# A selective scan in four directions: where the transposed delta, the row and column sums and their timing come from

## The chip, the cores and the metric

The kernel is one launch of a program for one NeuronCore of a Trainium2 chip. It runs four layers, one after the other. The metric is the device time of that launch in microseconds (us). Two lengths occur below: the time of an execution as it is measured, and the span of the profile, from the first instruction to the last. The engines are named as in the profile: PE (TensorE, with PEld for its weight loads), DVE (VectorE), ACT (ScalarE), POOL (GpSimd) and SP (SyncE, which here only issues DMAs).

## The reference, cut to what matters

Only layer 0 is touched. Its input has B = 4 images of 64 x 64 tokens with 128 channels. A projection gives 2 x 256 channels; a depthwise 3 x 3 convolution with silu gives `xa`; from `xa` come a small rank-8 input of delta and 16 values B and C for each token. Then a selective scan runs over the 4096 tokens in four orders:

```python
x_t = jnp.transpose(xa, (0, 2, 1, 3)).reshape(b, L, D_INNER)
xs = jnp.stack([x_flat, x_t, jnp.flip(x_flat, 1), jnp.flip(x_t, 1)], axis=1)
...
delta = jax.nn.softplus(delta + delta_bias[None, :, None])
...
def step(h, inp):
    u_i, d_i, b_i, c_i = inp
    dA = jnp.exp(d_i[..., None] * A)
    h = h * dA + (d_i * u_i)[..., None] * b_i[:, None, :]
    y = jnp.einsum('gdn,gn->gd', h, c_i)
    return (h, y)
```

`u` is `xs`, so the inputs differ by order; delta, B and C are the same four times, in row order. The four results are turned back to image order and added, `4 * D * xa` is added, and a layer norm over the 256 channels, a product with `silu(z)` and an output projection follow. DI = 256 channels are two halves h of 128; NST = 16 states; TC = 64 tokens are a chunk, so that one image row or column is a chunk and there are 64 chunks.

## The kernel before, in words

The work on an image has stages, written as Python generators that can be run alone or a step (up to the next `yield`) at a time. `front` (L283) normalizes the input and applies the input projection; it sends the padded convolution input and silu(z) to DRAM. `middle` (L358) does, for each block of 512 tokens, the convolution of both halves (L369, from tiles that `shifted` loads, L346), the transposes of its result (L387), the projection to the rank-8 input, B and C (L402), B in token order (L417, L422) and delta with softplus (L428 to L446), and sends all that to DRAM. `back` (L450) reads the summed scans of a block, adds the row and column sums (L468), normalizes (L475 to L497), multiplies by silu(z) (L501) and projects out (L508, L512).

The scans are one loop of N = 512 chunks (L749): image b, half h of the channels, chunk c. 64 chunks, one image's half, are called a unit here. Image 0 goes through front and middle before the loop (L724, the prologue). Inside the loop the stages of the other images run beside the scans: from chunk c = 4 of h = 0, a generator chain runs `back` of the image before (at image 0 instead `spectra`, which prepares tables for a later layer), `front` of the next image, then, not before h = 1, `middle` of the next image. Each chunk calls `next(beside)` twice, after its first and after its second half. At c = 59 of h = 1 what is left of the chain is run to its end at once (L762, L763), because the next image's loads begin.

A chunk holds four scans: kp = 0 for row order, kp = 1 for column order, and j for forward and backward. Its two halves are kp = 0 and kp = 1. For each half:

- `products` (L631) multiplies the transposed delta times input, `du`, with a diagonal of B, `dg`, into two PSUM tiles `db` (three such tiles exist). Sixteen matmuls.
- `scan` (L645): for each j, DVE adds the carried state into the first column (L650) and runs the recurrence over 16 states x 64 tokens into `st`, a buffer of tag `big` of which three exist (L653). Then POOL makes the carry for the next chunk (L661) and multiplies the states by C in place (L669).
- `total` (L676) sums over the states on PE, with the 0/1 matrix `both`, in two parts of four states pairs, into `yp` (L682). After part 1, ACT copies the four results into `yr` (row orders) and `yc` (column orders), each 128 x 4096 (L701). In the later half of a unit, when a place has been written once, what lies there is first added by an identity matmul (L694). Rows go to DRAM from SP (L706); columns are added onto `y0` in DRAM by two accumulating DMAs of POOL at the unit's end (L710).

`du` needs delta in token order, times `xT`, which `fetch` (L565) reads from DRAM two chunks ahead into `xo`. Delta itself is read by channel (`dl`, L536), ACT reverses it (L599), PE transposes both (L617) into half of the PSUM tile `aux`, and two DVE operations multiply (L628).

The order on PE, ACT and DVE is the order of the program (`manual_schedule`, L748). For PE a chunk I is: products of its first half, `total(I - 2, 1)`, a background step, products of its second half, the delta transposes of chunk I + 1, a background step, `total(I - 1, 0)`. For DVE: two adds and scans of the first half, DVE work of a background step, `du` of the next chunk, two adds and scans of the second half, DVE work of a background step. On POOL every half's L661 and L669 stand in the same order with L550 (the first decay of a chunk, once in four chunks), L468, L501 and L710 between them.

Of the kernel before, what the change touches and what calls it, by code (L numbers as in the profile page):

```python
# [14 lines left out]
P = 128  # L15
B = 4
HW = 64
# [142 lines left out]
def layer0(cm, x, W, x1, also, kept):  # L160
# [5 lines left out]
    with ExitStack() as ctx:  # L166
# [4 lines left out]
        t4 = ctx.enter_context(tc.tile_pool(name="l0t4", bufs=4))  # L171
        p2 = ctx.enter_context(tc.tile_pool(name="l0p2", bufs=2))
# [32 lines left out]

        both = tl(wp, [P, TC], "both")
# [27 lines left out]

        yr = tl(wp, [P, S], "yr")
        yc = tl(wp, [P, S], "yc")

        aux = tl(pp, [P, 2, 2, P], "aux")
        yp = aux[:, 0].rearrange("p k (j t) -> p k j t", t=TC)
        pt2 = aux[:, 1]  # L240
# [19 lines left out]
        def begin(b):  # L260
            img[b] = {
                "zs": tl(dr, [P, 2, S], "zs"),
                "dl": tl(dr, [2, P, S], "dl_d"),
                "ct": tl(dr, [NST, S], "ct_d"),
                "xT": tl(dr, [2, S, P], "xT_d"),
                "y0": tl(dr, [P, 2, S], "y0_d"),
                "yr": tl(dr, [P, 2, S], "yr_d"),
            }
# [77 lines left out]
        def shifted(i, pool, tag):  # L346

            k, h = divmod(i, 2)
            x3 = tl(pool, [3 * CG, 4, 8 * PADW], tag, bufs=None if tag == "big" else 1)
            for dy in range(3):  # L350
                s0 = (8 * k + dy) * PADW
                nc.sync.dma_start(
                    x3[dy * CG : (dy + 1) * CG],
                    xc_d[4 * h : 4 * h + 4, :, s0 : s0 + 8 * PADW].rearrange("g p s -> p g s"),
                )
            return x3

        def middle(b, bank, pool, tag, ahead):  # L358

            ready = [shifted(i, pool, tag) for i in range(ahead)]  # L360
            for k in range(NBLK):
                cols = slice(k * BLK, (k + 1) * BLK)
                xa = []
                for h in range(2):
                    ps = bank()
                    x3 = ready.pop(0)
                    for dx in range(3):
                        for g in range(4):
                            nc.tensor.matmul(  # L369
                                ps[g * CG : (g + 1) * CG, :], lhsT=cdiag[:, 4 * h + g, dx, :],  # L370
                                rhs=x3[:, g, 0 : 8 * PADW].rearrange(
# [24 lines left out]
                    if h == 0:  # L396
                        yield
                        yield
# [49 lines left out]
                yield  # L448
# [82 lines left out]
        def load(q):  # L531
# [3 lines left out]
            dl = tl(p2, [P, QC * TC], "dl")  # L535
            nc.sync.dma_start(dl, img[b]["dl"][h, :, cols])  # L536
# [6 lines left out]
            return {"dl": dl, "dp": dp, "dA": dA[q % 2], "h": h}  # L543
# [21 lines left out]
        def fetch(I):  # L565
# [9 lines left out]
            xo = tl(p2, [P, 2, P], "xo", bufs=3)  # L575
            xT = img[b]["xT"][h]
# [12 lines left out]
            inp[I] = {"ct": ct, "xo": xo, "dg": dg}  # L589
# [4 lines left out]
        def start(I):  # L594
            b, h, c = place(I)
            q = {"c": c, "h": h, "w": quads[I // QC], **inp.pop(I)}
            dlc = q["w"]["dl"][:, c % QC * TC : (c % QC + 1) * TC]
            dlr = tl(p2, [P, TC], "dlr")
            nc.scalar.copy(dlr, dlc[:, ::-1])  # L599
            q["dl"] = dlc, dlr  # L600
            return q
# [11 lines left out]
        def delta(q):  # L613

            pt = pt2[:, q["c"] % 2]
            for j in range(2):
                nc.tensor.matmul(  # L617
                    pt[j * TC : (j + 1) * TC, :], lhsT=q["dl"][j], rhs=cm.ident,
                    start=True, stop=True,
                )  # L620
            q["pt"] = pt

        def inputs(q):

            q["du"] = []
            for kp in range(2):
                d_ = tl(p2, [P, P], f"du{kp}")
                nc.vector.tensor_tensor(d_, q["xo"][:, kp, :], q["pt"], ALU.mult)  # L628
                q["du"].append(d_)

        def products(q, kp):  # L631
            bs = [tl(db, [P, 2 * NH0, TC], "db") for _ in range(2)]
            for g in range(2):
                for j in range(2):
                    half = slice(j * TC, (j + 1) * TC)
                    for p in range(2):
                        nc.tensor.matmul(  # L637
                            bs[j][p * TC : (p + 1) * TC, g * NH0 : (g + 1) * NH0, :],
                            lhsT=q["du"][kp][half, g * TC : (g + 1) * TC],
# [5 lines left out]
        def scan(I, q, kp, bs, st, old, new):  # L645
            c = q["c"]
            for j in range(2):
# [11 lines left out]
            us = slice(2 * kp, 2 * kp + 2)  # L659
# [16 lines left out]
        def total(I, part):  # L676
            b, h, c = place(I)
            st = states[I]
            late = c >= NCHUNK // 2
            for n in range(4 * part, 4 * part + 4):  # L680
                for p in range(2):
                    nc.tensor.matmul(  # L682
                        yp[p * TC : (p + 1) * TC], lhsT=both,
                        rhs=st[:, :, p * NH0 + n, :], start=(n == 0),
                        stop=(n == NH0 - 1 and not late),
# [3 lines left out]
            vs = [views(yc if kp else yr, c)[2 * j + kp] for j in range(2) for kp in range(2)]  # L689
            for j in range(2 if late else 0):  # L690

# [1626 lines left out]
```

## Time and profile before

| what | value |
|---|---|
| three runs | 10992.04, 11000.42, 11008.0 us; median 11000.42 |
| the profiled execution | 10974.05 us, span 10972.3 us |
| mean granted TensorE clock | 0.898 |
| first scan starts, last scan starts | 281.70 us, 6368.6 us |
| busy over the span | PE 9474.1, DVE 7569.2, POOL 5331.9, ACT 5425.1 us |
| busy from 280 to 6385 us | PE 5453, DVE 5423, POOL 5080, ACT 3066 us |
| HBM read, written | 667.01 MB, 331.61 MB |

The loop of layer 0 fills slices 2 to 23 of the page's 40. A line of the page's fifth part reads: source line, engine, operation, output <- inputs by the program's names with shapes, count | busy us, mean ns of one | idle us of that engine just before them, and what ended most of it. A line of the timeline reads: start, length, engine, source line, operation, names, shapes, count, and in brackets the idle time before it and what ended it.

### The profile page before, as it was taken

To read this page: it belongs to the slowest core of one execution; us is meant where nothing else is said; L and a number is where in the kernel's file an instruction comes from. 1 tells how busy PE (TensorE), PEld (TensorE's weight loads), DVE (VectorE), ACT (ScalarE), POOL (GpSimd) and SP (SyncE) were. 2 spreads that over 40 slices of the span, in tenths; PEclk is the share of its full clock that TensorE was granted. 3 is DMA by queue.
4 is the path that set the end of the run, shared out by engine and by line. 5 is a ranking of instruction groups with operands and counts; after the bars stand their busy time and mean duration, and the time that the engine had idled before them with its cause. 6 is when DMAs were issued, how large, how long until landed. Compare 5 with 4: busy or idle time off the path is not lost. (4 is left out here: it accounts for less than half of the span.)

```text
span 10972.3 us, 163387 instructions
## 1 busy us (share of the span) xinstructions
PE 9474.1 (86%) x59368; PEld 4529.1 (41%) x59368; DVE 7569.2 (69%) x11174; ACT 5425.1 (49%) x13536; POOL 5331.9 (49%) x2581
## 2 busy tenths in 40 slices
PE   6789998889998899998889954999999956988886
PEld 2344444344443344443344432444444434544442
DVE  1898988888988898988899966545452122355546
ACT  6666543555544564545542223777776622433321
POOL 0788888878888888887889940000000000000000
PEclk7899999999999899998999977999999976677777
DMA  5334443334443334443333341111100065022101
GB/s 147 106 107 149 131 128 114 109 109 149 136 132 116 107 117 151 135 122 113 109 106 99 103 120 36 41 35 35 39 24 17 16 191 104 17 46 56 37 24 46
DMA packets 1471160, 1009.46 MB, mean 92 GB/s; under 512 B 697540, under 2 KB 1296296, under 8 KB 1466008
## 3 DMA queue, kind: packets, MB, share of 16 engines
q1 hardware_dynamic: 1468056, 982.24, 30.3%
q0 software_dynamic: 2304, 16.78, 0.7%
q8 instruction: 475, 7.78, 0.3%
q14 instruction: 325, 2.66, 0.1%
HBM read 667.01 MB, written 331.61 MB: 91 GB/s over the span
## 5 line engine op out<-in xcount | busy, mean ns | idle before, releaser
L653 DVE TENSOR_TENSOR_SCAN big<-dA,db 128x1024 f32<-128x1024 f32 x2048 | 4680.0, 2286 | 82.1 <-ACT dA L560 3.2
L669 POOL TENSOR_TENSOR big<-big,ct 128x2048 f32<-128x2048 f32 x1024 | 4646.1, 4537 | 85.0 <-DVE big L653 5.4
L637 PE MATMUL db<-dg,du 64*64 64x512 f32 x16384 | 2442.7, 617 | 101.1 <-DVE db L650 87.8
L682 PE MATMUL aux<-big,both 128*64 128x256 f32 x16384 | 2104.0, 401 | 407.1 <-DVE db L650 260.6
L682 PEld LDWEIGHTS aux<-big,both 128*64 128x64 f32 x16384 | 1202.8, 142 | 1396.1 <-issue 622.9
L701 ACT COPY yr<-aux 128x64 f32<-128x64 f32 x1024 | 226.6, 222 | 2668.6 <-PE aux L694 1250.7
L637 PEld LDWEIGHTS db<-dg,du 64*64 64x64 f32 x16384 | 748.2, 135 | 1321.2 <-issue 1218.4
L608 ACT ACTIVATE dg<-mask,BT 128x64 f32<-128x64 f32 x4096 | 1007.4, 341 | 4.0 <-DMA dg_d<-dg 4.0
L1441 PE MATMUL av<-e,x 128*128 128x512 f32 x2048 | 974.0, 592 | 4.6 <-ACT e L1436 4.6
L1392 PE MATMUL qk<-a,xT 128*128 128x512 f32 x2048 | 966.6, 594 | 8.6 <-ACT e L1396 7.8
L1396 ACT ACTIVATE e<-qk,nk 128x512 f32<-128x512 f32 x1024 | 692.9, 685 | 539.2 <-PE qk L1392 538.4
L560 ACT ACTIVATE dA<-dp,A 128x252 f32<-128x252 f32 x2048 | 870.5, 509 | 1.4
L971 POOL TENSOR_TENSOR g_rs<-g_rs,qrow 128x4 f32<-128x4 f32 x32 | 41.1, 1285 | 1499.9 <-DVE g_rs L970 1499.9
L661 POOL TENSOR_TENSOR cy<-big,a 128x32 f32<-128x32 f32 x1008 | 272.8, 271 | 821.7 <-DVE big L653 524.4
L1392 PEld LDWEIGHTS qk<-a,xT 128*128 128x128 f32 x2048 | 378.0, 190 | 462.3 <-issue 358.0
L1441 PEld LDWEIGHTS av<-e,x 128*128 128x128 f32 x2048 | 381.6, 190 | 434.7 <-issue 393.6
L1436 ACT ACTIVATE e<-e 128x1024 f32<-128x1024 f32 x510 | 538.7, 1056 | 15.3
L1917 ACT ACTIVATE e<-s 72x576 f32<-72x576 f32 x448 | 273.3, 642 | 492.0 <-PE s L1910 489.0
L628 DVE TENSOR_TENSOR du<-xo,aux 128x128 f32<-128x128 f32 x1024 | 248.2, 284 | 379.5 <-PE aux L617 286.2
L650 DVE TENSOR_TENSOR db<-db,cy 128x16 f32<-128x16 f32 x2016 | 336.9, 167 | 202.0 <-PE db L637 184.2
L1928 POOL COPY vp<-vt 72x160 f32<-72x160 f32 x56 | 19.6, 352 | 890.8 <-PE po L1934 874.4
L2150 DVE SCALAR_TENSOR_TENSOR tex<-x,gw,tex 128x128 f32<-128x128 f32 x768 | 264.5, 344 | 256.1 <-PE x L2144 241.2
(525 smaller groups left out, 10869.4 us busy)
## 6 DMA issues: line engine op xcount, KB each, us to landing
ct<-ct_d SPq DMA_DIRECT2D x1024, 128.0 KB
dg_d<-dg SPq DMA_DIRECT2D x256, 512.0 KB
dg<-dg_d SPq DMA_DIRECT2D x256, 512.0 KB
xo<-xT_d SPq DMA_DIRECT2D x2048, 32.0 KB
x<-xc_d SPq DMA_DIRECT2D x144, 264.0 KB
dp<-dl_d SPq DMA_DIRECT2D x256, 128.0 KB
t2k<-in_x SPq DMA_DIRECT2D x96, 256.0 KB
sp<-sp_d SPq DMA_DIRECT2D x16, 1280.0 KB
```

What stands on the lines that cost most here:

```text
L560: nc.scalar.activation(w["dA"][:, :, g, n, 1:], w["dp"][:, g, :, 1:], AF.Exp, scale=A[:, w["h"], g, n : n + 1],)
L608: nc.scalar.activation(q["dg"][:, n, :], mask, AF.Copy, scale=BT[:, q["c"], n : n + 1])
L637: nc.tensor.matmul(bs[j][p * TC : (p + 1) * TC, g * NH0 : (g + 1) * NH0, :], lhsT=q["du"][kp][half, g * TC : (g + 1) * TC], rhs=q["dg"][ha ...
L650: nc.vector.tensor_tensor(bs[j][:, :, 0], bs[j][:, :, 0], old[:, u, :], ALU.add)
L653: nc.vector.tensor_tensor_scan(st[:, u].rearrange("p n t -> p (n t)"), q["w"]["dA"][:, c % QC].rearrange("p g n t -> p (g n t)"), bs[j].re ...
L669: nc.gpsimd.tensor_tensor(sv, sv, q["ct"].rearrange("p n t -> p (n t)").unsqueeze(1) .to_broadcast([P, 4, NH0 * TC]), ALU.mult,)
L682: nc.tensor.matmul(yp[p * TC : (p + 1) * TC], lhsT=both, rhs=st[:, :, p * NH0 + n, :], start=(n == 0), stop=(n == NH0 - 1 and not late),)
L1392: nc.tensor.matmul(ps, lhsT=me["xT"][:, kt * P : (kt + 1) * P], rhs=me["a"][k], start=True, stop=True,)
L1396: nc.scalar.activation(e[:, j, :], ps, AF.Exp, bias=me["nk"][:, kt : kt + 1], scale=2.0)
L1436: nc.scalar.activation(es[g + 2], es[g + 2], AF.Exp)
L1441: nc.tensor.matmul(avs[b, k], lhsT=img[b]["x"][:, kt, :], rhs=e[:, j, :], start=(kt == 0), stop=(kt == NT - 1),)
L1917: nc.scalar.activation(e.rearrange("p j h q -> p j (h q)"), ss[p][0:HALF, :, 0 : 2 * WIN], AF.Exp, scale=0.5,)
```

## The change

- `middle` makes delta in token order itself: after softplus, four transposes, a copy by ACT and a store to a new DRAM tensor `dT`; a matmul with `flip` reverses the tokens within each chunk, with another copy and store for the backward scans. A block has 15 steps instead of 12 (two empty steps and the last one are dropped).
- `fetch` reads `dT` into `dt`, with two DMAs; the load of `dl`, ACT's reversal, the transposes and their PSUM tile are gone. `du` of both halves is one DVE operation of 2 x 128 elements, with `dt` repeated over kp.
- `yr` and `yc` of 4096 tokens become `ys`: two buffers each of eight rows at either end, and of half a unit's columns. They are stored every eight chunks (rows) and every 32 (columns). In the later half of a unit POOL's accumulating DMAs add the rows in DRAM, as they do for the columns; the identity matmuls are gone.
- Both parts of `total(I - 2)` run in chunk I, each half a chunk later than before.
- The convolution's input comes in two tiles of half the size (of the tag `t4k`), two steps ahead, with six DMAs for three; the chain beside the scans starts at c = 5 instead of 4; `spectra` uses part of `padded[0]` as its input tile.

```diff
+        yb = ctx.enter_context(tc.tile_pool(name="l0y", bufs=2))
...
+        flip = tl(wp, [P, P], "flip")
+        nc.vector.memset(flip, 0.0)
+        for p in range(2):
+            half = slice(p * TC, (p + 1) * TC)
+            nc.vector.tensor_copy(flip[half, half], cm.ident[half, half][:, ::-1])
...
-        yr = tl(wp, [P, S], "yr")
-        yc = tl(wp, [P, S], "yc")
-
-        aux = tl(pp, [P, 2, 2, P], "aux")
-        yp = aux[:, 0].rearrange("p k (j t) -> p k j t", t=TC)
-        pt2 = aux[:, 1]
+        yp = tl(pp, [P, 2, 2, TC], "yp")
...
+                "dT": tl(dr, [2, 2, S, P], "dT_d"),
...
-            x3 = tl(pool, [3 * CG, 4, 8 * PADW], tag, bufs=None if tag == "big" else 1)
+            x3 = [tl(pool, [3 * CG, 2, 8 * PADW], tag) for _ in range(2)]
...
-                    if h == 0:
-                        yield
-                        yield
...
                     nc.sync.dma_start(img[b]["dl"][h, :, cols], r)
-                yield
+
+                    yield
+                    ps = bank()
+                    for i in range(4):
+                        nc.tensor.transpose(
+                            ps[:, i * P : (i + 1) * P], r[:, i * P : (i + 1) * P], cm.ident
+                        )
+                    for j in range(2):
+                        t = tl(tmp, [P, 4, P], "t2k")
+                        nc.scalar.copy(t, ps.rearrange("p (t c) -> p t c", c=P))
+                        nc.sync.dma_start(
+                            img[b]["dT"][h, j, cols, :].rearrange("(t p) c -> p t c", p=P), t
+                        )
+                        yield
+                        if j == 0:
+                            ps = bank()
+                            nc.tensor.matmul(
+                                ps, lhsT=flip, rhs=t.rearrange("p t c -> p (t c)"),
+                                start=True, stop=True,
+                            )
...
-            dl = tl(p2, [P, QC * TC], "dl")
-            nc.sync.dma_start(dl, img[b]["dl"][h, :, cols])
...
+            dt = tl(p2, [P, P], "dt", bufs=3)
+            nc.sync.dma_start(
+                dt[0:TC], img[b]["dT"][h, 0, c * TC : (c + 1) * TC, :]
+            )
+            nc.sync.dma_start(
+                dt[TC:P], img[b]["dT"][h, 1, c * TC : (c + 1) * TC, :]
+            )
...
-            q["du"] = []
-            for kp in range(2):
-                d_ = tl(p2, [P, P], f"du{kp}")
-                nc.vector.tensor_tensor(d_, q["xo"][:, kp, :], q["pt"], ALU.mult)
-                q["du"].append(d_)
+            q["du"] = tl(p2, [P, 2, P], "du")
+            nc.vector.tensor_tensor(
+                q["du"], q["xo"], q["dt"].unsqueeze(1).to_broadcast([P, 2, P]), ALU.mult
+            )
...
+            if part == 0:
+                if c % 8 == 0:
+                    for i in range(2):
+                        ys[i] = tl(yb, [P, 8 * TC], f"yr{i}")
+                if c % (NCHUNK // 2) == 0:
+                    ys[2] = tl(yb, [P, HW, TC], "yc")
...
-            for j in range(2 if late else 0):
-
-                for kp in range(2):
-                    v = vs[2 * j + kp]
-                    nc.tensor.matmul(
-                        yp[:, kp, j, :], lhsT=cm.ident, rhs=v[:, ::-1] if j else v,
-                        start=False, stop=(j + kp == 2),
-                    )
...
+            if r == 7:
+                for i, r0 in enumerate((c - 7, NCHUNK - 1 - c)):
+                    to = img[b]["yr"][:, h, r0 * TC : (r0 + 8) * TC]
+                    if c < NCHUNK // 2:
+                        nc.sync.dma_start(to, ys[i])
+                    else:
+                        nc.gpsimd.dma_start(to, ys[i], accum_op=ALU.add)
+            if c % (NCHUNK // 2) == NCHUNK // 2 - 1:
...
-                if h == 0 and c == 4:
+                if h == 0 and c == 5:
...
-                            middle(b + 1, own_bank, p2, "x3", 1),
+                            middle(b + 1, own_bank, t4, "t4k", 2),
...
                 if I > 1:
-                    total(I - 2, 1)
+                    total(I - 2, 0)
...
                 if nxt:
-                    delta(nxt)
                     inputs(nxt)
                 scan(I, now, 1, bs, st, carry, new)
...
-                if I:
-                    total(I - 1, 0)
+                if I > 1:
+                    total(I - 2, 1)
```

## The prediction

> **What bounds the kernel now.** I read the page's groups first, for the loop of layer 0 (512 chunks; first scan 281.7 us, last ends 6370.9, so 6089 of the 10972 us span). Only this loop and the prologue before it change.
>
> ```profile
> L653 DVE TENSOR_TENSOR_SCAN big<-dA,db 128x1024 f32<-128x1024 f32 x2048 | 4680.0, 2286 | 82.1 <-ACT dA L560 3.2
> L669 POOL TENSOR_TENSOR big<-big,ct 128x2048 f32<-128x2048 f32 x1024 | 4646.1, 4537 | 85.0 <-DVE big L653 5.4
> ...
> L628 DVE TENSOR_TENSOR du<-xo,aux 128x128 f32<-128x128 f32 x1024 | 248.2, 284 | 379.5 <-PE aux L617 286.2
> ```
>
> A chunk needs four scans on DVE and two multiplies on POOL, and the two engines are almost equally full. Then the waits inside the loop (engine and line, waited for: us, times, longest):
>
> ```profile
> DVE du L628 <- PE aux L617: 286.2, 265, 15.1
> DVE db L650 <- PE db L637: 184.2, 62, 17.9
> ```
> ```profile
> PE aux L682 <- POOL big L669: 112.5, 23, 7.5
> ```
> ```profile
> ACT yr L701 <- DMA yr_d<-yr: 69.7, 6, 21.0
> ```
>
> So DVE loses about 600 us to lateness of others, and L628, the line that changes, is where most of it shows. Next the timeline of a chunk with nothing beside it:
>
> ```profile
> 6001.43 4.53 POOL L669 TENSOR_TENSOR big<-big,ct 128x2048 f32<-128x2048 f32 x1
> ...
> 6003.59 2.29 DVE L653 TENSOR_TENSOR_SCAN big<-dA,db 128x1024 f32<-128x1024 f32 x1
> ...
> 6005.95 0.26 POOL L661 TENSOR_TENSOR cy<-big,a 128x32 f32<-128x32 f32 x1
> ...
> 6006.03 0.48 DVE L628 TENSOR_TENSOR du<-xo,aux 128x128 f32<-128x128 f32 x2 [0.15 <-PE aux L617]
> 6006.29 4.52 POOL L669 TENSOR_TENSOR big<-big,ct 128x2048 f32<-128x2048 f32 x1
> 6006.43 0.18 DVE L650 TENSOR_TENSOR db<-db,cy 128x16 f32<-128x16 f32 x1
> ```
>
> Starts to starts: add and scan 2.40 us, four of them 9.60; the two du 0.40; waits 0.25: a quiet chunk takes 10.29 (3 to 62 of the last unit of 64). POOL's pair L661, L669 runs back to back in 4.83 (6001.08 to 6005.95 is one of them), 9.66 a chunk. When DVE reaches du, POOL is still in L669 of the half before, by some 0.2 us.
>
> [...] Today du reads one operand from PSUM. After the change both lie in SBUF. The trace agrees, with a group that has two SBUF inputs already:
>
> ```profile
> 394.30 4.50 POOL L669 TENSOR_TENSOR big<-big,ct 128x2048 f32<-128x2048 f32 x1
> ...
> 395.55 3.53 DVE L862 SCALAR_TENSOR_TENSOR t4k<-t4k 128x256 f32<-128x256 f32 x1
> ...
> 399.01 0.17 DVE L650 TENSOR_TENSOR db<-db,cy 128x16 f32<-128x16 f32 x1
> ```
>
> L862 has 256 elements and takes 3.52 to 3.73 us all eight times, ending 0.27 us after POOL's multiply. [...] L856, the same shape with POOL free, takes 399 to 422, and DVE's next one starts 0.32 after it. [...] here L710 keeps POOL 0.86 to 1.19 us each.
>
> **The change part by part** (64 chunks are a unit, eight units).
>
> Delta from memory: four PE transposes (0.37 us of PE), one ACT copy and the wait L617 go. SP gets two issues a chunk for dt and loses one per four chunks. xo's four take 2.5 to 5.5 us of SP in the timeline, so two more of the same size take 1.2 to 2.8; in a quiet chunk SP stands idle 2.8 (6013.54 to 6016.32). They are asked for two chunks ahead, so I take nothing; uncovered they cost what xo costs du now, 22 us. In the middle SP also gets three more loads per half block and four stores of dT a block, behind which the fetches of later chunks are queued; they have the same chunk of room. One du of 256 elements for two: 0.40 to 0.32.
>
> The lock, quiet chunk: du right behind a scan waits for the end of L669 (0.2) and 0.2 to resume. Following both engines round from a du that ends at 0: DVE is back at the next du at 9.6; POOL starts its first multiply at 0.27, the second pair follows at 0.27 + 4.83, its end is at 9.6 or little after, and du resumes 0.2 behind it and takes 0.2: 10.05. POOL's L550 (0.41, once in four chunks) now delays du too: 10.1 against 10.29. A price of nothing would be 9.97.
>
> The lock, behind other DVE work: where a background operation stands between the second scan and du, POOL has started its next multiply.
>
> ```profile
> 2452.64 0.67 DVE L291 BATCH_NORM_STATS2 gn_st<-bg 128x6 f32<-128x512 f32 x1
> 2452.80 0.26 POOL L661 TENSOR_TENSOR cy<-big,a 128x32 f32<-128x32 f32 x1 [0.51 <-DVE big L653]
> 2453.14 4.54 POOL L669 TENSOR_TENSOR big<-big,ct 128x2048 f32<-128x2048 f32 x1
> 2453.23 0.47 DVE L628 TENSOR_TENSOR du<-xo,aux 128x128 f32<-128x128 f32 x2
> ```
>
> Here du, reading PSUM, runs through the multiply; with two SBUF inputs it would stand until 2457.7, 4.65 in all. I count 12 such places each for L291 and L512, 12 for L480 (4.07 left), 4 for L865/L868 (4.65). L291 and L512 miss the gap by 0.02 to 0.09 us only, so I take half of theirs. Three softplus operations (2.1) fall there in 20 of the new blocks of 15 steps (12 steps before): 3.1 each.
>
> POOL's debts. POOL's delays no longer spread over half a chunk: du hands them to DVE. In "back", per block of 512 tokens, L468 waits for its load (up to 4.7) and takes 2.36: 2.4 on DVE; with that debt open L480 costs 3.3 more in the other half of cases; L501 3.0. Per block: own DVE work 6.7 + 2.4 + 3.7 + 1.2 + 0.3 + 3.0 = 17.3. The sums, put half a chunk later, take away what costs as much today: PE waiting for L669 (some 5 us a block), with the products of the next chunk queued behind it and DVE behind those. Nothing takes its place on PE: L669 has half a chunk more. If POOL were a whole half behind, the wait would be back. The scans' third buffer is now free only after the last sum, but the products of the same chunk stand behind that sum on PE anyway.
>
> Sums in memory: yr, yc get two buffers. The stall at each unit's third chunk (24 to 28 us instead of 10; the seven du waits of 12.6 to 15.1) goes, 99 us, and so do the late ident matmuls L694 (1.06 of PE a chunk). But 64 row transfers move from SP to POOL, and 16 more of yc: 80 x 1.1 = 88, all before a du; where the middle runs POOL has slack: 70. L669 and L661 queue behind them.
>
> Middle: two more transposes and a flip per half, PE 14 us per 7.5 chunks instead of 11 per 6, the same density. Convolution 2.72 + sums 1.88 + products 1.88 exceed DVE's 4.8 plus du by 1.3, twice a block (today 1.8 to 2.9). 10.1 + (4.5 DVE + 2.6)/7.5 = 11.05 a chunk.
>
> The burst: the middle has 15 steps x 8 blocks = 120 instead of 96, and a chunk takes two. Back (89 steps) begins at chunk 5, front has 51, so in units 3 and 5 the middle begins at chunk 11; by chunk 59, where the loop at L763 empties the rest at once, 96 steps are done and 24 are left, in series through one PSUM bank. One softplus chain is 9.2 us in the prologue's timeline (L428 at 238.6 to L446's end at 247.8), and about 3.8 for transposes, copy, flip and copy: two of them 26. A whole block adds convolutions 2 x 6, and 5 to 6 for L402 and L417: 44. Together 70, and 5 for waits between them: 75, with DVE and POOL empty; 5 more for the slow PE after it (PE's twelve matmuls take 3.68 instead of 1.95 us after a gap). Unit 1 has two steps left, 5.
>
> Now the units, after against before (unit lengths from first scan to first scan). Unit 0: 8 quiet chunks 81, spectra 404 (392 now, less 0.2 a chunk, plus its four locks), front 272: 757 to 763. Unit 1: 59 middle chunks 652, softplus locks 25, burst 5, 5 quiet chunks: 732 to 747. Units 2 and 4: 5 quiet chunks 50, 45 of back 454 and 8 x 17.3 = 138, front 151: 794 to 811 and 807; 6, without front, 784 to 791. Units 3 and 5: 11 chunks 111, 48 of middle 549 with locks, burst 80, 5 chunks 50: 790 to 746 and 750. Unit 7: 64 quiet ones, 646 to 674. Sum 6087 against 6089. Then POOL's transfers +70, the prologue +36 (its ACT, 18.6 us busy of 24.7 a block, gets four copies of 0.56, and the softplus chain grows; between 18 and 80), one more sum after the last chunk +2. That is +108 on the profiled execution's 10974.05 (span 10972.3 and 1.75 around it): 11082. The median of the runs stands 26 above it: **11108**.
>
> **Rivals.** A, on the other side: du is let in. If the lock waits behind background work don't happen[...], the terms for L291, L512, L480, spectra and softplus go, 190 us: 10918. It decides at the order of du and L669 after a scan; for it speaks the margin of under 0.1 us, against it L862. C: the lock costs nothing anywhere, nor do debts pass through it: 6 to 7% of the loop, 10640; L862 speaks against. B: worse than forecast: all of L291 and L512 (+56), bursts of 100 (+40), prologue at its upper bound (+44): 11250.
>
> **How the numbers follow.** Forecast 0.58, A 0.22, C 0.04, B 0.16. About 0.2% (22 us) can be told from no change. A and C are faster, 0.26; of the forecast 0.08 falls within 0.2%; slower 0.66. The range leaves out C and a little at either end: 10890 to 11270.
>
> **What would show it.** Right: du waiting on POOL L669 instead of PE, single du of 3 to 5 us behind L291, L480, L442; quiet chunks of 10.1; no stall at a unit's third chunk; a hole of 75 us in the scans at chunk 59 of units 3 and 5; POOL DMA issues x96. Wrong: quiet chunks at 9.97 or above 10.3, du under 0.5 us behind background work, no hole.

## The result, and the profile after

The changed kernel takes 11441 us (median of 4 runs, 11427 to 11461); the kernel before took 10998 on the same chip (4 runs). The ratio is 1.040, 95% interval 1.038 to 1.042: slower by 443 us. The prediction had 11108 with a range of 10890 to 11270. The direction was right, the size a quarter of what came.

Nearly all of it lies where the change is. The first scan comes at 406.1 us instead of 281.7 (+124, forecast +36), and the loop takes 6422 us instead of 6089 (+333, forecast +70). What follows the loop takes 4603 against 4601.

The groups of the page of after (out<-in, busy us, mean ns of one, idle time ahead and what ended most of it). Scan and multiply are what they were; du is 546 us instead of 248, though half as many:

```profile
L663 DVE TENSOR_TENSOR_SCAN big<-dA,db 128x1024 f32<-128x1024 f32 x2048 | 4679.5, 2286 | 86.1 <-PE db L646 7.7
L678 POOL TENSOR_TENSOR big<-big,ct 128x2048 f32<-128x2048 f32 x1024 | 4652.7, 4544 | 107.6 <-PE db L646 27.3
...
L636 DVE TENSOR_TENSOR du<-xo,dt 128x256 f32<-128x256 f32 x512 | 546.2, 1067 | 34.0 <-DMA xo<-xT_d 16.7
```

The waits of after inside the loop, to be set against those of before. du's 286 us of waits for PE are gone, but L660, one step further down VectorE's queue, waits 417 instead of 184 for the products:

```profile
DVE db L660 <- PE db L646: 417.0, 175, 16.8
...
PE db L646 <- DMA dg<-dg_d: 118.4, 28, 12.3
PE bg L453 <- DVE t2k L447: 116.5, 30, 8.1
...
PE yp L698 <- ACT yc L712: 72.9, 31, 6.6
...
DVE db L660 <- POOL cy L670: 53.6, 13, 12.1
```

In the page's way of attributing, PE is late for three reasons that the forecast had at nothing: a load of dg that lands late, transposes of dT behind VectorE's softplus, and the sums behind ScalarE's copies.

A fourth stands in the groups of the page. The same 16384 products take PE 2809 us instead of 2443 (after, then before):

```profile
L646 PE MATMUL db<-dg,du 64*64 64x512 f32 x16384 | 2809.2, 649 | 602.9 <-DVE db L660 453.1
```
```profile
L637 PE MATMUL db<-dg,du 64*64 64x512 f32 x16384 | 2442.7, 617 | 101.1 <-DVE db L650 87.8
```

The granted TensorE clock over the loop is 0.905 in after and 0.951 in before (0.929 in e1 and 0.955 in e11 below). In these two traces it is either full or half. 1624 of the products of after begin at half clock, 631 of those of before; at half clock one takes 1057 ns (median), at full clock 589. Where the clock fell, PE had mostly stood: it was busy 33% of the 4 us ahead of such a fall in after (mean of 146), and 86% of the whole loop; in before 31% (67 falls) and 89%. So in these traces waits of PE are followed by slower products. The prediction had this cost for the holes only (5 us); what it makes of the 443 was not measured apart.

A quiet chunk of unit 7, in the timeline of after. From the scan at 6500.86 to the one four scans on, at 6511.04, it is 10.18 us (median of the unit 10.12, forecast 10.1); du takes 0.64 because it stands until 0.28 after the end of POOL's multiply:

```profile
6498.89 4.54 POOL L678 TENSOR_TENSOR big<-big,ct 128x2048 f32<-128x2048 f32 x1
...
6500.86 2.29 DVE L663 TENSOR_TENSOR_SCAN big<-dA,db 128x1024 f32<-128x1024 f32 x1
...
6503.07 0.64 DVE L636 TENSOR_TENSOR du<-xo,dt 128x256 f32<-128x256 f32 x1
6503.38 0.45 POOL L670 TENSOR_TENSOR cy<-big,a 128x32 f32<-128x32 f32 x1
```

Where a background operation stands between the second scan and du, POOL has begun its next multiply, and du stands through it, as forecast. Here L293 (L291 of before) is that operation. du ends at 2674.18, 0.29 after L678:

```profile
2668.80 0.70 DVE L293 BATCH_NORM_STATS2 gn_st<-bg 128x6 f32<-128x512 f32 x1
...
2669.36 4.53 POOL L678 TENSOR_TENSOR big<-big,ct 128x2048 f32<-128x2048 f32 x1
2669.42 4.76 DVE L636 TENSOR_TENSOR du<-xo,dt 128x256 f32<-128x256 f32 x1
2674.10 0.17 DVE L660 TENSOR_TENSOR db<-db,cy 128x16 f32<-128x16 f32 x1
```

And the hole at the 59th chunk of unit 3: three stretches of after by busy time of PE, its weight loads, VectorE, ScalarE and POOL. In the middle one the steps that are left run in series, and VectorE works 8.94 of 80 us. Unit 5 has the same hole.

```profile
3471.00:3555.00 84.00, 75.31 (x554) 31.71 (x554) 76.45 (x70) 35.02 (x82) 68.03 (x31) 0.96 0.46 129
3555.00:3635.00 80.00, 39.59 (x144) 13.38 (x146) 8.94 (x15) 35.05 (x48) 6.45 (x5) 0.55 0.36 106
3635.00:3700.00 65.00, 62.87 (x428) 24.29 (x426) 64.17 (x56) 25.09 (x99) 58.58 (x26) 1.00 0.27 79
```

The units against what the prediction gave them (us from first scan to first scan; the last runs to the end of the loop; the forecast's +70 for POOL's transfers isn't in its units):

| unit | 0 | 1 | 2 | 3 | 4 | 5 | 6 | 7 |
|---|---|---|---|---|---|---|---|---|
| before | 763 | 747 | 811 | 746 | 807 | 750 | 791 | 674 |
| forecast | 757 | 732 | 794 | 790 | 794 | 790 | 784 | 646 |
| after | 804 | 775 | 845 | 855 | 828 | 860 | 800 | 655 |

Unit 7, with nothing beside it, is nearly right. Every unit with work beside it is 16 to 70 us above forecast, 3 and 5, where the middle runs, by most.

### The profile page after: what moved, and what is told of

It is laid out like the page before. It is cut to its first block, busy times and chain, and to the rows that moved or that the text cites. A ratio compares the mean times of both kernels' runs of the same rounds, so it can differ in the third digit from the quotient of the medians.

```text
span 11431.0 us, 156940 instructions
## 1 busy us (share of the span) xinstructions
PE 9610.5 (84%) x55656; PEld 4238.1 (37%) x55656; DVE 7843.6 (69%) x10665; ACT 5419.6 (47%) x13149; POOL 5455.5 (48%) x2661
## 5 line engine op out<-in xcount | busy, mean ns | idle before, releaser
L678 POOL TENSOR_TENSOR big<-big,ct 128x2048 f32<-128x2048 f32 x1024 | 4652.7, 4544 | 107.6 <-PE db L646 27.3
L646 PE MATMUL db<-dg,du 64*64 64x512 f32 x16384 | 2809.2, 649 | 602.9 <-DVE db L660 453.1
L698 PE MATMUL yp<-big,both 128*64 128x256 f32 x16384 | 2188.0, 413 | 81.8 <-ACT yc L712 72.9
L698 PEld LDWEIGHTS yp<-big,both 128*64 128x64 f32 x16384 | 1175.3, 147 | 1450.1 <-issue 832.3
L712 ACT COPY yr<-yp 128x64 f32<-128x64 f32 x1024 | 224.9, 220 | 1670.4 <-PE yp L698 1669.7
L670 POOL TENSOR_TENSOR cy<-big,a 128x32 f32<-128x32 f32 x1008 | 341.6, 339 | 1250.3 <-DVE big L663 945.1
L660 DVE TENSOR_TENSOR db<-db,cy 128x16 f32<-128x16 f32 x2016 | 334.5, 166 | 472.1 <-PE db L646 417.0
L636 DVE TENSOR_TENSOR du<-xo,dt 128x256 f32<-128x256 f32 x512 | 546.2, 1067 | 34.0 <-DMA xo<-xT_d 16.7
```

Source lines behind the costliest of these rows:

```text
L636: nc.vector.tensor_tensor(q["du"], q["xo"], q["dt"].unsqueeze(1).to_broadcast([P, 2, P]), ALU.mult)
L646: nc.tensor.matmul(bs[j][p * TC : (p + 1) * TC, g * NH0 : (g + 1) * NH0, :], lhsT=q["du"][half, kp, g * TC : (g + 1) * TC], rhs=q["dg"][ha ...
L678: nc.gpsimd.tensor_tensor(sv, sv, q["ct"].rearrange("p n t -> p (n t)").unsqueeze(1) .to_broadcast([P, 4, NH0 * TC]), ALU.mult,)
L698: nc.tensor.matmul(yp[p * TC : (p + 1) * TC], lhsT=both, rhs=st[:, :, p * NH0 + n, :], start=(n == 0), stop=(n == NH0 - 1),)
```

## Experiments

The theory after this reading: the loss is the sum of several separate things that "delta by way of memory" brings: the lock on du (a du of over 1 us ends only 0.28 to 0.29 us after POOL's multiply beside it), DMA issues on SP's queue, work in series in the two holes and in the prologue, and PE waiting for VectorE's softplus. The rivals: that one of them is nearly all of it, or that they hide each other, since one late engine covers another. Most kernels undo one thing or leave one out; e5, e6 and e11 go back to delta by PE with the rest of the change kept, and e9 combines four repairs. Since the times of before differ by up to 0.3% from chip to chip, the column to read is the difference to the kernel before on the same chip.

| run | us | before there | difference | ratio, 95% | first scan | loop |
|---|---|---|---|---|---|---|
| after | 11441 | 10998 | +443 | 1.038 to 1.042 | 406 | 6422 |
| e1, du reads PSUM | 11175 | 10986 | +189 | 1.016 to 1.020 | 409 | 6141 |
| e2, no dT made beside the loop | 11352 | 10986 | +366 | 1.032 to 1.035 | 412 | 6323 |
| e3, a quarter of the dt loads | 11268 | 10986 | +281 | 1.024 to 1.029 | 402 | 6248 |
| e4, sums at their old place | 11461 | 10986 | +475 | 1.041 to 1.045 | 405 | 6455 |
| e5, delta by PE, sums at their old place | 10882 | 10977 | -94 | 0.988 to 0.993 | 302 | 6000 |
| e6, delta by PE, first in the chunk | 11096 | 10977 | +119 | 1.007 to 1.012 | 303 | 6215 |
| e7, steps spread | 11342 | 10977 | +365 | 1.030 to 1.035 | 409 | 6309 |
| e8, prologue in another order | 11320 | 10977 | +343 | 1.028 to 1.032 | 321 | 6403 |
| e9, four repairs | 10923 | 11008 | -85 | 0.988 to 0.994 | 319 | 6006 |
| e10, dt loaded in pairs | 11322 | 11008 | +314 | 1.025 to 1.032 | 414 | 6310 |
| e11, delta by PE, after the first products | 10697 | 11008 | -310 | 0.969 to 0.975 | 283 | 5786 |
| e12, e5 with the old tiles in the prologue | 10898 | 11008 | -110 | 0.986 to 0.992 | 283 | 6006 |

**The lock.** ScalarE copies the delta tile into PSUM:

```diff
+            q["pt"] = pt2[:, c % 2]
+            nc.scalar.copy(q["pt"], q["dt"])
...
-                q["du"], q["xo"], q["dt"].unsqueeze(1).to_broadcast([P, 2, P]), ALU.mult
+                q["du"], q["xo"], q["pt"].unsqueeze(1).to_broadcast([P, 2, P]), ALU.mult
```

> The changed kernel, but ScalarE copies each chunk's transposed delta tile from SBUF into a PSUM bank, and du reads it from there: du has one SBUF input again, everything else of the change stays. Theory [...]: the single du of 3 to 5 us behind background VectorE work disappear, du falls from 546 us in all to about 230, and the whole kernel takes 11441 - (270 to 340), about 11130. Rival (the lock only takes up time in which VectorE would wait for PE or GpSimd anyway): du gets just as short, the waits of L660 grow by as much, and the time falls by less than 100 us, above 11340.

Measured: +189 instead of +443, 254 less. The tile view of du (shortest, median and longest of one in ns) of after and then of e1:

```profile
L636 DVE TENSOR_TENSOR du<-xo,dt x512: 361/521/4784, 378.9 to 6813.2; 128x256 f32<-128x256 f32 x171
```
```profile
L641 DVE TENSOR_TENSOR du<-xo,aux x512: 360/395/423, 382.3 to 6535.1; 128x256 f32<-128x256 f32 x171
```

Same shape, same count, same neighbours: with one operand in PSUM none takes over 423 ns. All 512 take 204 us instead of 546, so 342 us of lock stood on VectorE, and the kernel became 254 shorter. Most of the rest came back as waits at the add behind du (L660 of after): for PE 446 us instead of 417, for POOL 104 instead of 54. By units: 0, 2, 4 and 6 (spectra, front, back) are 54 to 82 us shorter, 1, 3 and 5 (middle) only 7 to 16. There the rival holds: 63 us of these du stand behind softplus operations, and hardly any of it came out as time; that PE was late in those chunks anyway is argued, not shown. A quiet chunk is 9.93 us; the prediction gave 9.97 for a lock at no price.

**SP's queue.** Three quarters of the dt loads left out (du is then computed from the delta of other tokens), and, in another kernel, two chunks loaded by one DMA pair:

```diff
+            if c % QC == 0:
+                kept["dt"] = tl(p2, [P, P], "dt", bufs=3)
...
+            dt = kept["dt"]
```
```diff
+            if c % 2 == 0:
+                two["dt"] = tl(p2, [P, 2, P], "dt")
+                for j in range(2):
+                    nc.sync.dma_start(
+                        two["dt"][j * TC : (j + 1) * TC],
+                        img[b]["dT"][h, j, c * TC : (c + 2) * TC, :]
+                        .rearrange("(k t) d -> t k d", t=TC),
+                    )
+            dt = two["dt"][:, c % 2, :]
```

> The changed kernel with the two dt loads issued at every fourth chunk only; the other three chunks use the same tile again, so their du is computed from the wrong tokens' delta. It takes 768 DMA issues and 50 MB off SP's queue and nothing else. Theory (SP's queue is full wherever front, back and middle issue too, and what is late behind it stops PE and ScalarE): waits of PE for dg_d (118 us) and of SP for ct fall, and the time falls by 60 to 130 us, about 11340. Rival (the loads are asked for two chunks ahead and are covered, as the prediction had it): within 25 us of the changed kernel, above 11415.

> The changed kernel with dt loaded for two chunks at a time: half the DMA issues of dt on SP, the same bytes and the same number of 512-byte rows. It tells what the 174 us that three quarters of these loads cost are made of. If it is the issues on SP's queue: 384 issues of 768 saved in the other run's sense, about 90 less than the changed kernel, near 11350. If it is bytes and rows: within 25 us of the changed kernel, above 11415.

(The second text counts wrongly: of 1024 issues, pairs save 512, the quarter 768.) Measured: the quarter gains 162 us and the pairs, which move the same bytes and rows, 129. That is 0.21 and 0.25 us for each issue saved (with some 30 to 40 us of doubt in each difference, so the two agree): it is issues and not bytes. The quarter gains in the units with a middle (34, 44 and 50) and in unit 0 (20), less in 2, 4 and 6 (3 to 15). VectorE's wait for the products at L660 falls from 417 to 346 with the pairs and to 286 with the quarter. PE's wait for dg, which is loaded by the same queue behind dt and xo, falls too, but with the pairs by 27 us only, so it is not the whole way from the queue to the time; the lines of after (118.4, above), then of e10 and e3:

```profile
PE db L648 <- DMA dg<-dg_d: 91.6, 25, 15.0
```
```profile
PE db L647 <- DMA dg<-dg_d: 31.9, 11, 6.3
```

Why the two chunks of lead don't help is seen in SP's own timeline, in the middle of unit 3 of after (start, us that the issue takes, line, count):

```profile
3149.31 0.60 SPq L557 DMA_DIRECT2D dp<-dl_d  x1
3150.01 0.98 SPq L613 DMA_DIRECT2D dg<-dg_d  x1
3151.09 0.60 SPq L588 DMA_DIRECT2D ct<-ct_d  x1
3151.78 0.57 SPq L448 DMA_DIRECT2D dl_d<-t2k  x1
3152.40 0.57 SPq L588 DMA_DIRECT2D ct<-ct_d  x1
3153.07 0.65 SPq L595 DMA_DIRECT2D dt<-dT_d  x1
3153.81 0.54 SPq L459 DMA_DIRECT2D dT_d<-t2k  x1
3154.40 0.51 SPq L598 DMA_DIRECT2D dt<-dT_d  x1
3154.96 4.16 SPq L608 DMA_DIRECT2D xo<-xT_d  x3
3159.40 0.35 SPq L613 DMA_DIRECT2D dg<-dg_d  x1
3160.26 0.84 SPq L459 DMA_DIRECT2D dT_d<-t2k  x1
3161.15 0.51 SPq L608 DMA_DIRECT2D xo<-xT_d  x1
3161.75 1.03 SPq L719 DMA_DIRECT2D yr_d<-yr  x2
3162.87 1.43 SPq L588 DMA_DIRECT2D ct<-ct_d  x2
```

SP issues for 15 us with no gap above 0.55 us; a DMA of 32 KB (dt) costs it here as much as one of 256 KB (dT), 0.5 to 0.84 us, and three of xo's take 4.16. Unit 3 has 826 issues in after against 629 before (dt 130 of them). They don't fill it, since together they take 519 of its 855 us, but in stretches like this one the queue has no room. A load is asked for two chunks ahead, but issued when the queue comes to it: the second dt load here at 3154.40, 0.05 us after the issue of a store of dT ends.

**Making dT.** The transposes, the flip, their copies and stores left out for images 1 to 3:

```diff
                     yield
+                    if b:
+                        yield
+                        yield
+                        continue
```

> The changed kernel without the making of transposed delta beside the loop: for images 1 to 3 the middle leaves out the transposes, the flip, their copies and the stores of dT (its number of steps stays), and all loads of dt read the values of image 0. What it leaves out is part of the computation. It prices that work. Theory (PE waits for VectorE's softplus in L453, the dT stores queue ahead of loads on SP, and half of the emptied rest at the 59th chunk of units 3 and 5 is this work): the PE waits of L453 on L447 in the loop (116 us) go, the holes of 90 us shrink to about 60, the units with a middle are 25 to 60 us shorter, in all 120 to 200 less: about 11280. Rival (this work lies beside DVE's own): less than 60 saved, nearly all of it in the two holes, above 11380.

Measured: 77 us less, between theory and rival; the loop is 99 shorter. The chunk with the hole falls from 90.1 to 69.0 in unit 3 and 90.0 to 68.3 in unit 5, so 43 of it lie there. The waits of L453 on L447 (116.5) went with their instruction, but most of them had been covered, as it seems: units 1, 3 and 5, less the holes, are only 13 to 18 us shorter each.

**The holes.** A third step in every other chunk of units 3 and 5:

```diff
                 if beside:
                     next(beside, None)
+                    if b and h and 11 < c and c % 2 == 0:
+                        next(beside, None)
```

> The changed kernel with a third step of the work beside the loop in every other chunk from 12 on in units 3, 5 and 7 (24 more in a unit), so that nothing is left for the 59th chunk. Theory (the two holes of 90 us are work in series with empty engines, which costs a sixth of that beside the scans): the holes go, the middle chunks of units 3 and 5 get longer by 15 to 30 us a unit, and the whole is 110 to 150 us shorter than the changed kernel: about 11310. Rival (the middle is full on SP and PE already): the chunks get longer by most of the 90, and less than 50 are saved, above 11390.

Measured: 78 us less by the difference to before. The loop is 113 shorter, of which 31 lie in units whose code and steps are the same: so much is spread between runs. The same 80 us as above, from the start of the hole, in e7: VectorE works 73.84 of them instead of 8.94.

```profile
3555.00:3635.00 80.00, 72.71 (x479) 28.23 (x483) 73.84 (x67) 31.75 (x118) 72.68 (x35) 0.96 0.38 103
```

Units 3 and 5 are 39 and 43 shorter, not 80: the denser chunks give half of it back. So a hole of 80 us was worth 40.

**The prologue.** The turning of a block's delta is put behind the first convolution of the next block:

```diff
                     xa.append(xh)
+                    if late:
+                        turn(k - 1, late)
+                        late = []
                     yield
...
+                    if not b:
+                        late.append(r)
+                        continue
```

> The changed kernel with the prologue's order changed: for image 0 the transposes, flips, copies and stores of dT of a block come behind the first convolution of the next block, so that PE doesn't wait for VectorE's softplus before the second half's w_dt product and the next block. Nothing else. Theory (the prologue's 124 us are PE's order): first scan at 300 to 330 instead of 406, pitch of a block 27 to 30 us instead of 40, and the whole 75 to 105 us shorter, about 11350. Rival (the four more ScalarE copies and SP's stores set the pitch, not PE's order): pitch above 35, less than 45 us saved.

Measured: 100 us less, of which 86 at the first scan, now at 320.5. From block to block (L423) it is 40.5 us in after, 27.8 in e8, 25.0 before. Waits of the prologue, of after and then of e8; what PE waits for softplus falls from 120.7 to 48.8 (now at the convolution), and softplus's own wait for ScalarE falls by nearly half:

```profile
DVE db L443 <- ACT t2k L441: 130.5, 16, 12.3
...
PE db L453 <- DVE t2k L447: 120.7, 16, 8.6
```
```profile
DVE db L475 <- ACT t2k L473: 72.0, 16, 5.6
PE db L373 <- DVE t2k L479: 48.8, 14, 5.2
```

**The sums' place.** The sums alone put back:

```diff
-                    total(I - 2, 0)
+                    total(I - 2, 1)
...
-                if I > 1:
-                    total(I - 2, 1)
+                if I:
+                    total(I - 1, 0)
```

> The changed kernel with the sums over states where they were before the change: the second half of the sums of the chunk two back in the first half of a chunk, and the first half of the sums of the chunk just before at its end. Theory, as the prediction has it (the later sums save some 5 us a block of 512 tokens, where PE would stand behind GpSimd's multiply): 80 to 160 us slower, about 11560, with PE waits on L678 again. Rival (in the changed kernel the later sums stand behind ScalarE's copies L712 instead, 73 us of PE waits of L698, and give back what they save): within 40 us of the changed kernel or faster.

Measured: 32 us slower, as the rival had it, and no more than the sign is sure: the intervals of after and e4 (1.038 to 1.042, 1.041 to 1.045) meet. The later sums save 14 to 27 us in units 2, 4 and 6 and cost 2 to 12 in four of the others.

**Without the way by memory.** Everything of the change but that: delta transposed on PE into PSUM as before, one du for the pair, sums added in memory, sums at their old place:

```diff
-            q["du"] = []
-            for kp in range(2):
-                d_ = tl(p2, [P, P], f"du{kp}")
-                nc.vector.tensor_tensor(d_, q["xo"][:, kp, :], q["pt"], ALU.mult)
-                q["du"].append(d_)
+            q["du"] = tl(p2, [P, 2, P], "du")
+            nc.vector.tensor_tensor(
+                q["du"], q["xo"], q["pt"].unsqueeze(1).to_broadcast([P, 2, P]), ALU.mult
+            )
```

> The change without its delta from memory, and with the sums over states at their old place: the changed kernel with delta transposed on PE into PSUM as before (no dT stores, no dt loads, no flip, 12 steps a block, the step list begun at chunk 4), keeping the one du of a pair, which now reads PSUM, and the row and column sums added in memory. Theory (all of the loss comes from delta by way of memory: lock 266, SP and dT work 170, bursts 160, prologue 120; the rest of the change gains, since units 2, 4 and 6 of the kernel with du from PSUM are already 45 us shorter than before): first scan back at 282, no hole in units 3 and 5, and 100 to 180 us less than before, about 10850. Rival (GpSimd's 96 accumulating DMAs cost what the unit-start stalls cost before): within 40 us of before, 10950 to 11030.

Measured: 94 us faster than before, with all 96 accumulating DMAs on POOL. Against e4, which differs from it only by delta's way through memory and what goes with it, it is 569 less. So, undone in this order, the change's 443 is 569 for delta by way of memory, 94 back for what else the change has (one du, the sums in memory, the smaller convolution tiles), and 32 back for the later sums. In another order the shares can differ.

**The order on PE.** Two kernels with the later sums have the transposes of delta further ahead in PE's order. First at the start of the chunk, then behind the first products:

```diff
+                if nxt:
+                    delta(nxt)
                 bs = products(now, 0)
...
-                    delta(nxt)
                     inputs(nxt)
```
```diff
                 bs = products(now, 0)
+                if nxt:
+                    delta(nxt)
...
-                    delta(nxt)
                     inputs(nxt)
```

> As the kernel with delta by PE, but with the sums half a chunk later, as in the change, and with the transposes of delta for the next chunk issued on PE ahead of the first products of this chunk instead of behind the second [...]. du then waits for a result that is half a chunk old. Theory (the waits of du for the transposes, 286 us in 265 places before, are a matter of order on PE): du waits under 40 us in all, and 60 to 150 us less than the kernel with delta by PE at its old place, about 10740. Rival (PE is late by itself; what du no longer waits, L660 waits for the products): within 40 us of that kernel, and the waits of L660 on L646 larger by as much as du's are smaller.

> The kernel with delta by PE and the later sums again, but the transposes of delta stand between the first products and the sums of a chunk: there ScalarE's copies out of the shared PSUM bank (L700), for which the early transposes waited 603 us, are half a chunk old. Theory (what made the early place slow was that wait at the head of PE's queue, nothing else): no PE wait of L615 on L700 above 100 us in all, du without its 135 us of waits, and 30 to 90 us less than the kernel with delta by PE and sums at their old place, about 10820. Rival (ScalarE is so far behind beside front and middle that the copies are late there too): above 10920.

Measured: at the start 213 us slower than e5, which neither theory nor rival had; behind the first products 216 faster than e5, far below the time that was expected. e6 and e11 differ in this place alone, and it makes 429 us between them; against e5 both have the later sums as well. VectorE's waits in e5, e6 and e11, in this order:

```profile
DVE db L648 <- PE db L634: 252.9, 89, 16.5
DVE du L624 <- PE aux L615: 135.6, 257, 2.2
```
```profile
DVE db L648 <- PE db L634: 666.8, 549, 19.3
```
```profile
DVE db L648 <- PE db L634: 231.0, 150, 13.9
```

In both du no longer waits. The difference is what PE itself waits for, first in e6, then in e11:

```profile
PE aux L615 <- ACT yc L700: 603.5, 508, 9.0
```
```profile
PE aux L615 <- ACT yc L700: 78.9, 57, 6.5
```

In e6 each chunk begins, on PE, with a transposition that waits for ScalarE's four copies of the chunk before, and the products stand behind it. Both use the two halves of one PSUM tile; that this is why the transposition waits at all is argued from the names, and wasn't tried. Half a chunk later the copies are done. e11 is 2.85% faster than before (interval 2.5 to 3.2), the best kernel here. In unit 7 a chunk takes 9.93 us, and units 3 and 5 take 706 and 709.

**All repairs, and the tiles.** 

> The changed kernel with four repairs together, delta still by way of memory: du reads it from PSUM after a ScalarE copy, the third step in every other chunk (no rest at the 59th chunk), the prologue's transposes a block later, and the dt loads of two chunks in one DMA pair. Theory (the losses are separate and add up): 266 + 99 + 121 less than the changed kernel, and up to 60 for the loads, 10870 to 10955, about level with or just under before. Rival (they overlap: a chunk freed of the lock is then held by SP, and the third step meets a queue that is full): under 400 us gained, above 11040.

> The kernel with delta by PE and sums at their old place, with the convolution tiles of the prologue back in the big tiles (one load of three rows instead of two of each). Only the prologue differs. Theory (its first scan at 302 instead of 282 comes from the conv loads, six DMAs per half block through four small tiles): first scan at about 282, 20 us less, about 10862. Rival (it is something else, such as ScalarE): first scan at 300, no difference.

e9 (the edits of e1, e7, e8 and e10 in one) is 528 us below the changed kernel; the four alone gave 254, 78, 100 and 129, together 561. They add up: the losses are separate. It still stands 226 above e11; in the two traces 37 us of the difference are in the prologue, 40 in unit 1 and some 90 in each of units 3 and 5. These are the places where dT is still made and stored; no run leaves that out of e9.

e12 has its first scan at 282.5, but e11, with the small tiles, has it at 282.6, and e6, whose prologue is the same code as e11's, at 303.3. So the tiles are not the reason, and the theory falls. The same prologue takes 283 in one run and 303 in another. The traces show what differs: from 130 to 270 us the granted clock is 0.65 in e5 and 0.70 in e11. A block (L421) with some 20 us at half clock takes 27.1 to 27.3 us, most with 13 to 18 us of it take 23.5 to 24.9; of seven blocks e5 has five of the first kind, e11 one. Why the clock fell at other moments stays open.

## Why the prediction was wrong

By its own steps:

**Right in kind and size.** Quiet chunks 10.1. The lock behind background work: forecast some 190 us, measured 223 us in 62 du that have such work ahead of them, less 0.395 each for their own work, 199. The share for L291 and L512 was taken too small (half; 10 of 12 blocked each), L480 too large (2.7 us each and not 4.07), and softplus a little (2.8 and not 3.1). The holes: 75 and 5 forecast, 80 without a scan measured. The terms of du behind background work are thus not what failed.

**"They are asked for two chunks ahead, so I take nothing."** This step failed. It read the room on SP from a quiet chunk (2.8 us idle) and used it for chunks with the middle's loads and stores beside it, where SP has none for 15 us on end. "Uncovered they cost what xo costs du now, 22 us" was no bound: it asked what du would wait for, and what waits is PE, for dg behind the dt loads (118.4 us). The runs give 129 us for half of the dt issues and 162 for three quarters.

**"The prologue +36 (18 to 80)."** It measured +124 in the first scan. The sum counted ScalarE's copies and a longer chain, and not that L453 waits on PE, in order, for VectorE: from then on the second half's w_dt product and the next block's convolution stand behind it. Another order alone took 86 of it back.

**"Nothing takes its place on PE."** It did: PE waits 72.9 us for ScalarE's copies L712, which stand behind ScalarE's background work, and 116.5 for softplus at L453. The later sums are worth 32 us here, and not five in each of 24 blocks, 120; with delta on PE, the later sums and e11's order together are worth 216.

**"The middle ... the same density"** and "two more transposes and a flip": counted as PE time, 14 us per 7.5 chunks. Leaving that work out saved 77 us, 43 of them in the holes. The cost was where these instructions stand and not how long they take.

**Debts.** 49 du of over 1 us have nothing between the scan and them: 121 us, with POOL late from work of its own. Among POOL's eight instructions before them stand an accumulating DMA (26 of them, 50 us) or back's L488 or L521 (15, 50 us), and both of these debts are in the prediction. The other eight, 20 us, are not explained.

**The unit-start stall, -99.** This failed too. The second to eighth chunks of all units took 739 us before and take 727 in after, so 12 of the 99 came. The cause that the prediction saw is gone, but another wait stands in its place. Units 3 and 5 still stall at the third chunk (23.7 and 23.9 us) and unit 1 at the fourth (20.8), and there PE waits for dg (12.3, 11.2 and 10.7 us). Units 2, 4 and 6 stall at the fourth (22.9 to 23.8), where POOL waits for the load of yr (13 times, 82 us in all, 14.0 the longest). Only unit 7 has no stall. In e11 units 1, 3 and 7 have no early chunk above 17.1.

**POOL's accumulating DMAs, +70.** They take POOL 0.88 us each (median of 64) and 1.34 (of 32), 99 us, as forecast. What they cost in time wasn't measured alone; e5 is 94 faster with them.

**The sums.** The step to +108 leaves out that its units came to 2 us less than before; it should be +106. And L856, given as 399 to 422 ns, has a longest of 519. Neither matters.

The range failed as well as the number: its slow case B turned up terms that the forecast had already, and no case let a term at nothing be wrong. The part that was in doubt, the lock, was priced nearly right; of those put at nothing, SP's queue alone was worth 129 us and more. What these steps missed is together more than the 335 us that the forecast lacks, since each was measured or counted by itself; the runs don't divide the 335 among them.

## What to carry to other kernels

A queue has room only where it is read in the stretch concerned: count the issues of a new load in the busiest stage and not in the quiet one, since loads behind it can wait with it (here PE's waits for dg, which is loaded behind dt and xo, fell from 118 us to 32 with a quarter of the dt loads). And of each instruction added to an engine ask what it waits for and not how long it takes: on PE, the same two transposes of a chunk, put at its start or behind its first products, made 429 us between the two kernels. Where a VectorE operand can be had from PSUM, taking both from SBUF beside a busy GpSimd has a price of its own, here 254 us.

## What the runs showed that was not expected

- A VectorE multiply of 256 elements a partition takes 0.36 to 0.42 us with one operand in PSUM (all 512 of e1), and up to 4.78 with both in SBUF (after). There each of the 108 that take over 1 us ends 0.28 to 0.29 us after a multiply of GpSimd. Of 342 us so lost, 254 were time of the kernel.
- Issuing one dt load of 32 KB takes SP 0.51 and 0.60 us (medians of the two lines), and each one left out was worth 0.21 to 0.25 us of the kernel, whether its bytes were moved by another or not.
- The same prologue code took 20 us more in one run than in another, with more of it at half clock (from 130 to 270 us the granted clock was 0.65 in e5 and 0.70 in e11).
- In the loop 1624 products ran at half clock in after and 631 in before; PE's own waits stand ahead of these stretches (PE was busy 33% of the 4 us ahead in after, 31% in before).
